# First lists' products deferred, later lists a step later, residual loads on the stores' queue, the last block in pieces, more strip buffers: a graph layer on one Trainium2 core

## The chip, the cores and the metric

One core of a Trainium2 chip. The metric is device time of one execution in microseconds (us). The four executions of a kernel mostly lie within 1% of each other. Every experiment was checked against the reference (all correct) and timed in turn with the kernel before on the same chip. The experiments ran in five batches on five chips (median of before 1692.8 to 1701.8), so a difference of a few us across batches means little.

## The reference

```python
def reference(x, adj, W):                  # x (8, 4096, 256), adj (4096, 4096), W (256, 256), all f32
    A = relu((adj + adj.T) * 0.5)
    D = A.sum(axis=1)
    r = where(D > 0, D, 1) ** -0.5          # 0 where D is 0
    L = eye(4096) - r[:, None] * A * r[None, :]
    y = relu(einsum('nm,bmo->bno', L, einsum('bnf,fo->bno', x, W)))
    z = x + y
    return (z - mean(z)) / sqrt(var(z) + 1e-5)   # over the last axis
```

`adj` is sparse, so the kernel gathers only the rows it needs.

## The kernel before

Phase one goes over blocks of A (8 x 8 of 512 x 512): transpose, add, store to `a_dram`; between them `form(m)` makes G = r·xW for 128 rows. It also makes the first lists of gather indices. Phase two has 15 full units and a half one; a unit computes two blocks of 128 output rows, b0 and b1, with four PSUM banks each. Its products use gathered tiles of A (`ga`) and G (`g`). Each list is ready two units ahead.

```python
    # phase one, at the end of a row i of blocks (cut)
    for u in ([0], [1, 2], [3])[i]:
        patterns(u)                          # VectorE: kinds
        tot = psum.tile(..., tag="b0"); low = psum.tile(..., tag="b0")
        count(u, tot, low)                   # TensorE: products over kinds
        place(u, tot, low)                   # VectorE

    # form(m) (cut): all transposes and copies of a block first, then all its products
    for b in range(0, B, 2):
        ...transpose x[b], x[b + 1]; nc.scalar.copy(xt[:, b : b + 2], pt)
    for b in range(0, B, 2):
        ...products of xt with W

    # phase two (cut)
    def residual(i, ypool):
        xr = ypool.tile([P, B, F], F32, tag="xr", name=f"xr_{i}", bufs=4)
        nc.scalar.dma_start(xr, x[...block i...])
        return xr

    def finish(i):
        y = evict(i, py.pop(i), ypool)       # ScalarE: relu(-r * PSUM), four banks
        def rest():
            mv, rstd = moments(i, y, xr.pop(i), stat)     # VectorE: z = xr + y, statistics
            def end():
                normalise(i, z, mv, rstd)    # VectorE; then the store on SyncE's queue
                if i + 3 < NB:
                    xr[i + 3] = residual(i + 3, ypool)
            after(6, end)
        after(1, rest)

    def lists(u):
        one = psum.tile([P, S], F32, tag="b0"); two = psum.tile([P, S], F32, tag="b0")
        count(u + 4, ...); count_rest(u + 3, ...)
        collect(u + 2, pl); index(u + 2, pl)              # 32 small products; VectorE reads them
        place_rest(u + 3, ...); place(u + 4, ...)         # VectorE reads the rest of both banks

    for q, (u, step) in enumerate(steps):    # a step: the products of one or two gathered pairs
        ...
        finish(2 * u + 1 + b)                # when block b has had its last product
        if b == 0:
            after(2, lists, u)               # two steps later
```

The lists of a unit take two of the four `b0` banks, and the first products of the next unit need all four. A load of `xr` goes into the buffer of four blocks earlier and so waits for that block's store to land. VectorE does its work in program order, so an add that waits for a residual holds up the reads of the lists behind it.

## Time and profile before

| | before |
|---|---|
| median of 4 runs, us | 1696.8 (1692.9 to 1702.0) |
| first product of phase two | 630.8 |
| first list's products to the sixth's ("five units") | 740 to 1091: 351 us |
| first to last product of phase two | 1031 us |
| last product to the end | 29.5 us |

The times inside are from the timeline of the profiled run. "Five units" runs from the lists' products of unit 0 to those of unit 5.

### The profile page before, as it was taken

To read this page: it belongs to the slowest core of one execution; us is meant where nothing else is said; L and a number is where in the kernel's file an instruction comes from. 1 tells how busy PE (TensorE), PEld (TensorE's weight loads), DVE (VectorE), ACT (ScalarE), POOL (GpSimd) and SP (SyncE) were. 2 spreads that over 40 slices of the span, in tenths; PEclk is the share of its full clock that TensorE was granted. 3 is DMA by queue.
4 is the path that set the end of the run, shared out by engine and by line. 5 is a ranking of instruction groups with operands and counts; after the bars stand their busy time and mean duration, and the time that the engine had idled before them with its cause. 6 is when DMAs were issued, how large, how long until landed. Compare 5 with 4: busy or idle time off the path is not lost.

```text
span 1691.1 us, 18475 instructions
## 1 busy us (share of the span) xinstructions
PE 1517.8 (90%) x6544; PEld 802.7 (47%) x6544; DVE 802.6 (47%) x1831; ACT 360.7 (21%) x453; POOL 818.9 (48%) x1113
## 2 busy tenths in 40 slices
PE   6999779598898979999999999999997999988693
PEld 5887657486776723434343333333332333333231
DVE  4776676758455320051507154446436336415325
ACT  3655435354443510010100001001101101100110
POOL 3010010101011146667677777777777778768550
PEclk8999979799998989999999999999998999989897
DMA  9999979898997679989898999999998999999984
GB/s 334 375 383 388 387 279 393 305 396 323 335 323 257 235 283 401 353 300 359 334 358 316 380 354 366 389 359 352 372 359 296 383 348 350 353 369 339 332 334 152
DMA packets 229156, 575.13 MB, mean 340 GB/s; under 512 B 19913, under 2 KB 118521, under 8 KB 191385
## 3 DMA queue, kind: packets, MB, share of 16 engines
q0 software_dynamic: 56672, 305.12, 47.1%
q1 hardware_dynamic: 100352, 134.23, 23.0%
q10 hardware_dynamic: 72032, 134.51, 21.2%
q8 instruction: 55, 0.90, 0.2%
q14 instruction: 45, 0.37, 0.1%
HBM read 479.07 MB, written 136.34 MB: 364 GB/s over the span
## 4 chain that ended last, share of the span: by engine, by line
PE 38%; DMA 23%; issue 22%; DVE 11%; POOL 4%; ACT 1%; ACTq 0%; POOLq 0%; SPq 0%; DVEq 0%
PE py L693 15%; DMA out_dram<-xr 13%; PE pg L425 10%; DMA xr<-in_x_dram 9%; PE lead L396 6%; PE tr L341 4%; PE xtr L415 3%; DVE xr L536 2%; DVE xr L522 2%; DVE stats L527 2%; POOL ga L588 1%; DVE hot L263 1%; DMA g<-g_dram,gi 1%; POOL g L598 1%; DVE part L346 1%
## 5 line engine op out<-in xcount | busy, mean ns | idle before, releaser
L693 PE MATMUL py<-g,ga 128*64 128x512 f32 (+1 forms) x3152 | 959.2, 606 | 34.4 <-issue 15.6
L693 PEld LDWEIGHTS py<-g,ga 128*64 128x64 f32 (+1 forms) x3152 | 359.5, 155 | 622.2 <-issue 593.5
L598 POOL DMA_INDIRECT g<-g_dram,gi x302 | 358.8, 1188 | 188.0 <-PE py L693 76.3
L588 POOL DMA_INDIRECT ga<-a_dram,ai x302 | 333.1, 1103 | 100.0 <-issue 81.9
L522 DVE TENSOR_TENSOR xr<-xr,y 128x2048 f32<-128x2048 f32 x32 | 73.3, 2289 | 521.6 <-ACT y L512 300.3
L512 ACT ACTIVATE y<-py,minus_r 128x512 f32<-128x512 f32 x124 | 78.0, 687 | 964.7 <-PE py L693 428.4
L344 DVE TENSOR_TENSOR sym<-tr,adj 128x512 f32<-128x512 f32 x256 | 158.6, 681 | 209.0 <-PE tr L341 142.3
L425 PE MATMUL pg<-w_sb,xt 128*128 128x256 f32 x1024 | 232.1, 383 | 1.4 <-ACT xt L416 1.2
L425 PEld LDWEIGHTS pg<-w_sb,xt 128*128 128x128 f32 x1024 | 194.0, 193 | 32.1 <-ACT xt L416 4.2
L391 POOL DMA_DIRECT2D strip<-a_dram x32 | 18.7, 587 | 321.5 <-PE lead L396 302.5
L341 PE MATMUL tr<-ident,adj 128*128 128x128 f32 x1024 | 135.3, 288 | 30.0 <-DMA adj<-in_adj_dram 12.8
L346 DVE TENSOR_REDUCE part<-sym 128x32 f32<-128x2048 f32 x64 | 144.1, 2275 | 7.9 <-ACT sym L345 7.8
L345 ACT ACTIVATE sym<-sym 128x2048 f32<-128x2048 f32 x64 | 122.5, 1913 | 113.9 <-DVE sym L344 113.8
L341 PEld LDWEIGHTS tr<-ident,adj 128*128 128x128 f32 x1024 | 120.7, 148 | 44.3 <-issue 19.0
L536 DVE TENSOR_SCALAR xr<-xr,mv,rstd 128x256 f32<-128x256 f32 x256 | 86.7, 410 | 85.7 <-POOL rstd L534 85.7
L434 ACT ACTIVATE gt<-pg,r 128x512 f32<-128x512 f32 x96 | 66.0, 687 | 100.4 <-PE pg L425 100.3
L527 DVE BATCH_NORM_STATS2 stats<-xr 128x6 f32<-128x256 f32 x256 | 86.8, 410 | 0.7
L396 PE MATMUL lead<-gt,strip 128*128 128x512 f32 x192 | 86.5, 592 | 0.0
L366 POOL TENSOR_TENSOR r<-e,neg_half 128x4 f32<-128x4 f32 x8 | 8.3, 1043 | 154.9 <-DVE e L365 154.9
L416 ACT COPY xt<-xtr 128x512 f32<-128x512 f32 x128 | 67.8, 591 | 71.2 <-PE xtr L415 71.0
L415 PE MATMUL xtr<-ident,xin 128*128 128x128 f32 x512 | 73.7, 297 | 9.1 <-DVE sym L344 8.0
L534 POOL TENSOR_TENSOR rstd<-rstd,neg_half 128x8 f32<-128x8 f32 x32 | 59.0, 1843 | 33.9 <-DVE rstd L530 33.3
(100 smaller groups left out, 587.0 us busy)
## 6 DMA issues: line engine op xcount, KB each, us to landing
adj<-in_adj_dram SPq DMA_DIRECT2D x64, 1024.0 KB
a_dram<-sym ACTq DMA_DIRECT2D x64, 1024.0 KB
xin<-in_x_dram SPq DMA_DIRECT2D x32, 1024.0 KB
xr<-in_x_dram ACTq DMA_DIRECT2D x32, 1024.0 KB
out_dram<-xr SPq DMA_DIRECT2D x32, 1024.0 KB
g_dram<-gt ACTq DMA_DIRECT2D x24, 1024.0 KB
g_dram<-held ACTq DMA_DIRECT2D x8, 1024.0 KB
ga<-a_dram,ai POOLq DMA_INDIRECT x302
```

Of the source, the lines that this page charges most:

```text
L341: nc.tensor.transpose(pt[:, c * P : (c + 1) * P], tji[:, c, a * P : (a + 1) * P], ident)
L344: nc.vector.tensor_add(sym[:, a, :], pt, tij[:, a, :])
L345: nc.scalar.activation(sym, sym, AF.Relu, scale=0.5)
L346: nc.vector.tensor_reduce(part[:, i * A : (i + 1) * A, j * S // Q : (j + 1) * S // Q], sym.rearrange("p a (c q) -> p a c q", q=Q), AX.X, A ...
L396: nc.tensor.matmul(lead[c], lhsT=strip, rhs=g[:, c * S : (c + 1) * S], start=not done, stop=len(done) == NB - 1, skip_group_check=True,)
L415: nc.tensor.transpose(pt[:, k, c, :], xin[:, b + k, c * P : (c + 1) * P], ident)
L425: nc.tensor.matmul(pg[:, k * FO : (k + 1) * FO], lhsT=xt[:, b + k, c, :], rhs=w_sb[:, c, :], start=(c == 0), stop=(c == FC - 1),)
L527: nc.vector.bn_stats(stats[:, b, :], z[:, b, :])
L536: nc.vector.tensor_scalar(z[:, b, :], z[:, b, :], mv[:, b, 0:1], rstd[:, b : b + 1], ALU.subtract, ALU.mult,)
L588: nc.gpsimd.indirect_dma_start(out=at if both else at[:, :P], out_offset=None, in_=a_pairs if both else a_rows, in_offset=bass.IndirectOff ...
L598: nc.gpsimd.indirect_dma_start(out=gt, out_offset=None, in_=g_dram, in_offset=bass.IndirectOffsetOnAxis(ap=gi[:, t : t + 1], axis=0), boun ...
L693: nc.tensor.matmul(py[2 * u + 1 + b][c][rows, :], lhsT=at[:, off + rows.start : off + rows.stop], rhs=gt[:, c * S : (c + 1) * S], start=ne ...
```

## The change

Intent: TensorE shall not wait for the first lists' kinds at row ends (the products are put some blocks behind); ScalarE's evictions shall not stand behind residual loads that wait for stores (these loads go to SyncE, which issues the stores, and the lists come a step later); the tail shall overlap (four pieces); GpSimd shall fetch strips earlier (eight buffers). The diff, cut to its core:

```diff
-            t = xpool.tile([P, P], F32, tag="strip", name=f"strip_{m}", bufs=4)
+            t = xpool.tile([P, P], F32, tag="strip", name=f"strip_{m}", bufs=8)
...                                            # form(): transposes of b beside products of b - 2
-            for b in range(0, B, 2):
-                ...transposes, copy into xt[:, b : b + 2]
-            for b in range(0, B, 2):
+            xts = {}
+            for b in range(0, B + 2, 2):
+                if b < B:
+                    ...transposes
+                    xts[b] = xpool.tile([P, 2, FC, P], F32, tag="xt", name=f"xt_{m}_{b}", bufs=3)
+                    nc.scalar.copy(xts[b], pt)
+                b -= 2
+                if b < 0:
+                    continue
+                xt = xts.pop(b)
...                                            # after every block of A: run_due()
+                    due.append([2 + n, count_place, (u,)])
+                    due.append([1 + u, count_place_rest, (u,)])
+                due.append([2, collect_index, (i - 4,)])
...
-        nc.scalar.dma_start(xr, x[:, i * P : (i + 1) * P, :].rearrange("b p f -> p b f"))
+        nc.sync.dma_start(xr, x[:, i * P : (i + 1) * P, :].rearrange("b p f -> p b f"))
...
+            if i == NB - 1:
+                finish_last(i)                 # per PSUM bank: evict, add, statistics, normalise, store
+                return
...
-                        after(2, lists, u)
+                        after(3, lists, u)
```

## The prediction

> **What bounds the kernel now.** I read the page first, then the windows table in stretches of 100 and of 20 us, then the waits, and last the timeline around each gap. The kernel has two phases. Until about 620 us it symmetrises A, stores it, forms G = r·xW and makes the first index lists; after that it gathers rows of A and G with 302 pairs of indirect transfers and multiplies them. The windows (columns: TensorE, weight loads, VectorE, ScalarE, GpSimd busy; granted clock; DMA share; GB/s):
>
> ```profile
> 100.00:200.00 100.00, 96.20 (x546) 79.17 (x546) 64.66 (x88) 52.58 (x64) 8.77 (x17) 0.98 1.04 386
> 200.00:300.00 100.00, 78.75 (x436) 62.26 (x436) 68.92 (x99) 43.67 (x45) 6.48 (x13) 0.88 0.92 343
> 500.00:600.00 100.00, 93.22 (x464) 70.57 (x463) 41.75 (x63) 41.84 (x52) 13.71 (x26) 0.95 0.72 262
> 1000.00:1200.00 200.00, 197.89 (x810) 75.48 (x809) 89.79 (x267) 15.39 (x24) 154.30 (x130) 1.00 0.97 370
> 1400.00:1600.00 200.00, 167.53 (x596) 65.27 (x594) 88.36 (x266) 17.07 (x28) 145.34 (x121) 0.91 0.94 349
> ```
>
> TensorE and DMA are near their limits together. From 100 to 200 us TensorE is 96% busy and the DMA moves 386 GB/s; the best 20 us windows of the whole run show 400 to 409, and I use 392 as a sustained ceiling. From 380 to 620 us TensorE alone binds (262 GB/s). The middle of phase two has both full; its end (1400 to 1600) has 32 us without a matmul, at 349 GB/s. So the reader should see that a removed wait pays only where the other limit has room.
>
> The gaps of phase one are the ends of rows of blocks. There TensorE stands in program order before the count of a list:
>
> ```profile
> 209.54 2.48 DVE L344 TENSOR_TENSOR sym<-tr,adj 128x512 f32<-128x512 f32 x4 [3.17 <-DMA a_dram<-sym]
> 221.30 0.47 PE L206 MATMUL tot<-kind,ones 128*128 128x352 bf16 x1 [16.41 <-DVE kind L196]
> PE tot L206 <- DVE kind L196: 36.7, 4, 18.7
> ```
>
> VectorE itself was held by a full set of sym buffers whose stores had not landed, so the count's input came late. In phase two ScalarE's queue issues the residual loads, and each waits there until an output store has landed; the evictions behind it wait too:
>
> ```profile
> 1499.93 15.29 ACTq L506 DMA_DIRECT2D xr<-in_x_dram  x2
> 1515.33 2.42 ACT L512 ACTIVATE y<-py,minus_r 128x512 f32<-128x512 f32 x4 [54.19 <-DMA xr<-in_x_dram]
> 1516.06 0.18 PE L234 MATMUL lists<-rest,ones 128*128 128x32 bf16 x1 [7.42 <-ACT y L512]
> 1524.14 2.29 DVE L522 TENSOR_TENSOR xr<-xr,y 128x2048 f32<-128x2048 f32 x1 [36.43 <-DMA xr<-in_x_dram]
> 1530.54 44.64 PE L693 MATMUL py<-g,ga 128*64 128x512 f32 x128 [5.06 <-DVE pos_r L171]
> ```
>
> Two stalls in one unit: 7.4 us because the eviction stood behind the second load, and 5.1 us because VectorE, waiting for the first load to land, read the lists' PSUM late. The tail:
>
> ```profile
> 1661.88 0.37 ACTq L506 DMA_DIRECT2D xr<-in_x_dram  x1
> 1662.36 2.42 ACT L512 ACTIVATE y<-py,minus_r 128x512 f32<-128x512 f32 x4 [18.55 <-PEq L725]
> 1673.62 2.29 DVE L522 TENSOR_TENSOR xr<-xr,y 128x2048 f32<-128x2048 f32 x1 [9.70 <-DMA xr<-in_x_dram]
> 1681.22 2.67 DVE L536 TENSOR_SCALAR xr<-xr,mv,rstd 128x256 f32<-128x256 f32 x8 [1.82 <-POOL rstd L534]
> ```
>
> The last matmul ends near 1662.3 and the span 28.8 us later, of which 9.7 are the wait for the last residual.
>
> **What the Trainium skill says.** "DMA: Bandwidth & Descriptors", section "Queues, rings and completion order": SP and ACT own one row of rings each on the same 16 engines, and each engine takes turns between rows, packet by packet. The trace agrees in kind: a 1 MB output store alone on its row took 17.8 us (1482.1 to 1499.9) beside the gathers, far below an equal share of bytes. Section "Anatomy of one DMA — SWDGE (gpsimd) path": the wait for a semaphore happens on the issuing sequencer. The trace shows it, 15.3 us on ScalarE's queue. "TensorE: Matmul & The Clock Gate", section "What's actually happening": half clock after an idle window. After the stall ending at 1530.5 weight loads come every 0.86 us, and from 1536.4 every 0.43, so a stall costs about 3 us more than its length. "SBUF — State Buffer", section "SBUF: two separate sides": VectorE can lock GpSimd out of its port while descriptors are written. One gather issue took 4.47 us beside the 4.42 us hot comparison, 0.94 otherwise. The change leaves that as it is.
>
> **Part one: lists' products later.** Idle TensorE time at row ends, from the 20 us windows: row one (180 to 240 us) 20.9, row two (280 to 320) 18.7, rows three to five 5.3, 7.8 and 6.8. After rows one and two the DMA has to have room: 220 to 260 us ran at 197 and 345 GB/s, which against 392 is 9.9 + 2.4 = 12.3 us; 300 to 340 at 317 and 269, 3.8 + 6.3 = 10.1 us. In rows three to five TensorE binds and all 19.9 us could go. Cap: 42 us. I take 60%, 25 us: VectorE still waits for the sym stores, the four PSUM banks stay full until it has added, and a deferred count now takes two of these banks in the middle of a row. Against it stands the new order in form(): the first product follows two transposes, not four. The transpose began at 185.44 and ScalarE's first copy ended at 186.65, so the product can start at about 186.75, where the two transposes are through at 186.3: 0.44 us of idle per form. For some 18 forms after 380 us, where TensorE binds, that is 8 us. Net 17.
>
> **Part two: residual loads on SP; lists a step later.** In favour: the ScalarE stall goes. TensorE waited for evictions before lists 12.6 + 10.0 + 7.4 + 1.1 = 31.1 us, and each stall costs a ramp. But at the cited unit the second limit ends at the same 1530: VectorE has to have the residual first. It lands 24.2 us after issue, issue follows the store of four blocks earlier, and that follows a normalisation which stands behind the previous residual add in VectorE's order. This loop took 66 us from add to add (1476.6 to 1542.6); a unit has 57 us of DMA work (16 tiles of 1.13 MB and 4.2 MB at 392 GB/s). The change lengthens it: the instruction order of SP now reads store, load (waits for that store), store, load. A second store, formerly issued 5.6 us after the first, waits until the first has landed, about 12 us, and its load follows it on a row that moves about 60 GB/s under gathers. The loop becomes about 75 us where gathers keep running; when TensorE stalls they stop, and the row speeds up. I expect the first stall to go, the second to stay, and a few late units to gain or lose 3 us: 6 us won in the whole phase.
>
> **Part three: last block in pieces.** After the last matmul, for each of four pieces: eviction 0.69, add 0.57, two statistics 0.82, aggregate and epsilon 0.33, GpSimd power about 1.6 with its waits, two normalisations 0.67. VectorE's share of the four is about 10 us, and the order shows five of block 29's eight normalisations and all of block 30's behind it, 13 × 0.33 = 4.3 us, which formerly came ahead. Their stores, 2 MB, end the program: about 6 us. So 0.7 + 10 + 4.3 + 6 = 21, plus up to 4 us for a residual that still arrives late: 23 against 28.8. Gain 6.
>
> **Part four: eight strips.** GpSimd waited 302.5 us for a strip's slot, but it had nothing else to do; only at 602 us did the power of r stand behind strips, and TensorE lost 0.6 us. Worth 0 to 1.
>
> Sum: 1694.6 − 17 − 6 − 6 − 0.5 = **1665 us**, 1.7% less.
>
> **Rivals.** (a) Evictions were the real brake. ScalarE's waits on stores and residuals (235 and 203 us) speak for it, and the 54 us of idle TensorE in phase two with their ramps. Then phase two gains up to 35 us, limited by DMA, and the time is about 1636. Against: units late in the run already take 58 to 62 us by their evictions, near the 57 of DMA. (b) SP becomes the bound: stores and loads share one row and one waiting sequencer. Then the late units take 5 to 8 us more each, seven of them give back 40 us, and the time is about 1700. Against: the rows get faster whenever gathers pause. (c) DMA hides part one: the saved stalls of rows one and two return as waits for blocks of A. Then part one is worth 8 us and the time 1674.
>
> **Range and chances.** The parts' spreads are about 10, 18 and 5 us, together about 22 us; 80% is 1632 to 1692. The 2% line lies at 1660.7, a little under my middle: faster 0.45, same 0.50, slower 0.05.
>
> **What would show it.** Right: no TensorE wait of 16 us for a kind; phase two starting 12 to 22 us earlier; small TensorE waits for the xt copy at each form; evictions directly after their matmuls, with TensorE waits before products still on VectorE reads of lists, and SP issues held 10 us or more by stores; about 23 us after the last matmul. Wrong: late units under 56 us or over 66, a tail over 28, or a wait for blocks of A as long as the old one for kinds.

## More of the kernel before

Most of the reading is in the prediction; only the hardware queues are added here (packets, MB, share of the 16 engines' time; q10 holds ScalarE's transfers and q1 SyncE's):

```profile
q1 hardware_dynamic: 100352, 134.23, 23.0%
q10 hardware_dynamic: 72032, 134.51, 21.2%
```

## The result

After: 1761.97 us, median of 4 runs (1754.2 to 1765.0), against 1696.76 of the kernel before: ratio 1.0383 (1.0339 to 1.0428). It is 3.8% **slower**, and outside the range.

| | before | after |
|---|---|---|
| first product of phase two | 630.8 | 627.7 |
| five units | 351 | 369 |
| first to last product of phase two | 1031 | 1095 |
| last product to the end | 29.5 | 29.3 |

Phase one is 3 us shorter, the tail the same, and all the loss is in phase two. The page's queues show the loads moved over:

```profile
q1 hardware_dynamic: 133680, 167.78, 28.4%
q10 hardware_dynamic: 38752, 100.96, 14.7%
```

The waits of the kernel after (what waited, for what: us in all, times, longest), TensorE in phase two and then SyncE's queue over the run:

```profile
PE py L738 <- DVE pos_k L170: 35.2, 5, 13.7
PE py L738 <- DVE low L299: 17.9, 1, 17.9
PE py L738 <- DVE pos_r L245: 17.4, 1, 17.4
```

```profile
SPq L531 <- DMA out_dram<-xr: 409.8, 23, 41.1
```

The waits for evictions ahead of lists (31 us before) are gone, as intended, and so is the 36.7 us wait for kinds. In their place TensorE waits 76.1 us for VectorE's reads of the lists (70.5 in the rows shown, 5.6 in two smaller ones), against 15.1 before (8.3 for `pos_k`, 5.1 for `pos_r`, 1.7 for `low`). SyncE stands 410 us in front of residual loads, waiting for stores. One stall of after, in the timeline (start, duration, engine, what, and in brackets the idle time before it and what ended it):

```profile
1563.97 0.19 PE L234 MATMUL lists<-rest,ones 128*128 128x32 bf16 x1
1564.92 1.94 PE L738 MATMUL py<-g,ga 128*64 128x512 f32 x8
1569.89 3.61 PE L738 MATMUL py<-g,ga 128*64 128x512 f32 x6 [3.03 <-DVE pos_r L171]
1587.84 2.29 DVE L548 TENSOR_TENSOR xr<-xr,y 128x2048 f32<-128x2048 f32 x1 [18.00 <-DMA xr<-in_x_dram]
1590.05 0.17 DVE L298 COPY low<-lists 128x16 f32<-128x16 f32 x1
1590.87 4.67 PE L738 MATMUL py<-g,ga 128*64 128x512 f32 x14 [17.37 <-DVE pos_r L245]
```

Read it from below: TensorE's products waited 17.4 us for VectorE to read the lists, which stood behind an add, which waited 18 us for its residual. Four of TensorE's waits are of this kind, 52 us in all. Four others (1194 to 1388 us, 24 us in all) follow no late residual: there VectorE copies the list 8 to 10 us late, of which more below. The same list in the kernel before:

```profile
1517.59 7.89 PE L693 MATMUL py<-g,ga 128*64 128x512 f32 x24
```

Before, 24 products as the profile counts them (7.9 us) lay between the lists' products and the first product that needs their banks. After, 8 (1.9 us) do: "a step later" spends that slack. SyncE's order, in the same kernel:

```profile
1527.31 0.38 SPq L571 DMA_DIRECT2D out_dram<-xr  x1
1539.60 0.37 SPq L531 DMA_DIRECT2D xr<-in_x_dram  x1
1540.02 0.58 SPq L571 DMA_DIRECT2D out_dram<-xr  x1
```

The load of 1539.60 waited for a store to land, and the store of 1540.02 stood behind it, though its normalisation ended at 1534.9: the serialisation that the prediction had read from the instruction order.

### The profile page after: what moved, and what is told of

Read it like the earlier page. It is cut to its first block, busy times and chain, and to the rows that moved or that the text cites. A ratio compares the mean times of both kernels' runs of the same rounds, so it can differ in the third digit from the quotient of the medians.

```text
span 1752.4 us, 18499 instructions
## 1 busy us (share of the span) xinstructions
PE 1546.2 (88%) x6544; PEld 808.5 (46%) x6544; DVE 800.6 (46%) x1837; ACT 363.0 (21%) x453; POOL 812.9 (46%) x1116
## 4 chain that ended last, share of the span: by engine, by line
PE 60%; DMA 13%; issue 11%; DVE 10%; POOL 2%; ACT 2%; another core or an unknown queue 2%; SPq 0%; ACTq 0%; DVEq 0%; POOLq 0%
PE py L738 43%; PE pg L430 10%; DMA out_dram<-xr 7%; PE lead L396 4%; DVE sym L344 3%; DMA xr<-in_x_dram 2%; PE xtr L420 2%; ACT sym L345 1%; DVE part L346 1%; PE tr L341 1%; DVE xr L563 1%; DVE xr L548 1%; DVE stats L553 1%; DMA a_dram<-sym 1%
## 5 line engine op out<-in xcount | busy, mean ns | idle before, releaser
L738 PE MATMUL py<-g,ga 128*64 128x512 f32 (+1 forms) x3152 | 980.4, 608 | 104.4 <-DVE pos_k L170 35.2
L738 PEld LDWEIGHTS py<-g,ga 128*64 128x64 f32 (+1 forms) x3152 | 367.5, 155 | 708.9 <-issue 644.7
L625 POOL DMA_INDIRECT g<-g_dram,gi x302 | 374.2, 1239 | 257.2 <-PE py L738 167.8
L615 POOL DMA_INDIRECT ga<-a_dram,ai x302 | 316.8, 1049 | 101.5 <-issue 83.4
L548 DVE TENSOR_TENSOR xr<-xr,y 128x2048 f32<-128x2048 f32 (+1 forms) x35 | 73.7, 2105 | 490.4 <-ACT y L537 298.8
L430 PE MATMUL pg<-w_sb,xt 128*128 128x256 f32 x1024 | 253.0, 397 | 26.2 <-ACT xt L422 18.7
L344 DVE TENSOR_TENSOR sym<-tr,adj 128x512 f32<-128x512 f32 x256 | 162.4, 683 | 124.3 <-PE tr L341 108.5
L391 POOL DMA_DIRECT2D strip<-a_dram x32 | 17.4, 545 | 336.0 <-PE lead L396 328.4
L396 PE MATMUL lead<-gt,strip 128*128 128x512 f32 x192 | 92.2, 594 | 1.6 <-DMA strip<-a_dram 1.6
L422 ACT COPY xt<-xtr 128x512 f32<-128x512 f32 x128 | 73.3, 580 | 16.6 <-PE xtr L420 16.1
L420 PEld LDWEIGHTS xtr<-ident,xin 128*128 128x128 f32 x512 | 62.9, 145 | 29.9 <-DVE sym L344 17.3
```

What stands on the lines that cost most here:

```text
L344: nc.vector.tensor_add(sym[:, a, :], pt, tij[:, a, :])
L396: nc.tensor.matmul(lead[c], lhsT=strip, rhs=g[:, c * S : (c + 1) * S], start=not done, stop=len(done) == NB - 1, skip_group_check=True,)
L420: nc.tensor.transpose(pt[:, k, c, :], xin[:, b + k, c * P : (c + 1) * P], ident)
L430: nc.tensor.matmul(pg[:, k * FO : (k + 1) * FO], lhsT=xt[:, k, c, :], rhs=w_sb[:, c, :], start=(c == 0), stop=(c == FC - 1),)
L615: nc.gpsimd.indirect_dma_start(out=at if both else at[:, :P], out_offset=None, in_=a_pairs if both else a_rows, in_offset=bass.IndirectOff ...
L625: nc.gpsimd.indirect_dma_start(out=gt, out_offset=None, in_=g_dram, in_offset=bass.IndirectOffsetOnAxis(ap=gi[:, t : t + 1], axis=0), boun ...
```

## The experiments

Theory at the start: lists a step later and loads on SyncE, because of late residuals. Rivals: lists a step later by itself; SyncE's queue by itself; a slower TensorE. Labels with `a_` undo parts of after, with `b_` add parts to before; `d_only` is the kernel before with the deferral alone. All outputs are right.

### Undoing part two, half by half

```diff
 # a_act: after, loads back on ScalarE      # a_two: after, lists back at two steps
-        nc.sync.dma_start(xr, ...)          -                        after(3, lists, u)
+        nc.scalar.dma_start(xr, ...)        +                        after(2, lists, u)
 # a_act_two: both.   b_sp: before, with nc.sync.dma_start(xr, ...) alone
```

> The changed kernel with its residual loads back on ScalarE's queue, all else kept. Theory Q (the shared SP queue is the loss: a store waits in the queue until the load ahead of it may be issued, and its own load then comes later): about 1700 us, near the kernel before. Theory L (the lists a step later are the loss: their PSUM is read by VectorE behind the second residual add, and the next block's products wait for that): still about 1745 us. If the two feed one another, between the two.

> The changed kernel with the lists back at two steps after the block, residual loads still on SP. Theory Q: still about 1745 us, with second stores of a unit held behind loads. Theory L: about 1700 us, and no TensorE wait of 10 us or more for VectorE's reads of the lists. If they feed one another, both this and the ScalarE variant get back most of the 65 us.

> Both undone: the changed kernel keeps only the deferred first products, the reordered form, the strips and the last block in pieces. If the loss is all of phase two's, 1680 to 1700 us; with what I predicted of the first phase and the tail, about 1672 us. If it stays over 1730 us, neither Q nor L is the cause.

> The kernel before with the residual loads on SP alone. Theory Q: 1730 us or more. Theory L: 1690 to 1705 us. If the queue matters only together with the later lists, 1695 to 1715 us.

Measured (before 1701.75): a_act 1753.55 (1.0297), a_two 1709.31 (1.0009; median of its three fast runs), a_act_two 1703.26 (1.0003), b_sp 1720.3 (1.0085). So lists a step later cost 53 us (a_two to after) and 50 us (a_act_two to a_act); the loads on SyncE cost 8 (a_act to after), 6 (a_act_two to a_two) and 19 us (before to b_sp), by the ratios 15, 1 and 14, which is near the scatter. Neither half brings a gain.

The waits do not divide like the times. The largest of a_two, TensorE in phase two:

```profile
PE py L738 <- DVE pos_k L170: 40.3, 3, 20.7
PE py L738 <- DVE low L299: 25.8, 1, 25.8
```

In all TensorE waits for reads of the lists 5.8 us in a_act_two, but 70.6 in a_two, 66.3 in a_act and 89.1 in b_sp. Either half alone brings these waits, while only the step later costs some 50 us. So their sum is not the loss.

### The same halves from the other side, and the deferral alone

```diff
 # b_three: before, with
-                        after(2, lists, u)
+                        after(3, lists, u)
 # b_three_s6: b_three, and the even blocks' add put off so that VectorE reads the lists first
-            after(1, rest)
+            after(1 if i % 2 else 6, rest)
-                after(6, end)
+                after(6 if i % 2 else 1, end)
 # a_five: after, and
-  xr bufs=4;  ga in a pool of RING + 2
+  xr bufs=5;  ga bufs=RING
 # d_only: after with old form(), 4 strips, old tail, loads on ScalarE, lists at two
```

> The kernel before with the lists one step later, alone. From the first batch (the changed kernel lost about 50 us with the lists at three steps whichever queue the loads used) this should be 1745 us or so, with TensorE waits of 10 us and more for VectorE's reads of the lists in the late units. If it stays under 1710 us, the step costs only together with the rest of the change.

> As the run before, but the residual add of each unit's second block is put off (its normalisation stays where it was), so that VectorE's order reads the lists ahead of it, as in the kernel before; the lists are still a step later on TensorE. If the order on VectorE is what costs (reads of the lists behind a second wait for a residual), about 1700 us. If the later place on TensorE is what costs (no products between the lists and the next block), still about 1745 us.

> The changed kernel with five residual buffers in place of four (the small gathered tiles have 13 buffers in place of 15 to make room). A load then needs the store of five blocks earlier, which has long landed. If late residuals are the root of both losses, about 1700 us or less, with hardly any wait for residuals on VectorE. If the shared queue's bandwidth is the root, still about 1750 us.

> The kernel before with the deferred first products alone (old form, four strips, old tail, loads on ScalarE, lists at two). My first part said 25 us of the first phase for this alone: 1675 us, and first products of phase two at about 606 us against 630.8. If the blocks of A limit the rows' ends, or the reordered waits come back elsewhere, 1695 to 1700 us.

Measured (before 1698.24): b_three 1708.31 (1.0040), b_three_s6 1705.18 (1.0038), a_five 1701.28 (0.9994), d_only 1681.33 (0.9892). Lists a step later cost only 10 us on top of before, against some 50 in after, though TensorE waits 70.6 us for reads of the lists in b_three too. Putting the adds off changes nothing, but it is no test of VectorE's order, since the edit did not do what it was meant to: in the trace of b_three_s6 the copy of a late list still stands behind an add that waits for its residual, and TensorE's waits for the lists stay at 63.6 us:

```profile
1548.60 2.29 DVE L522 TENSOR_TENSOR xr<-xr,y 128x2048 f32<-128x2048 f32 x1 [13.12 <-DMA xr<-in_x_dram]
1550.81 0.17 DVE L298 COPY low<-lists 128x16 f32<-128x16 f32 x1
```

A fifth residual buffer takes back all 60 us, but not by making the residuals early: with the loads on SyncE, VectorE's adds still wait 130 us for them (after 128) and TensorE 70.8 us for the lists. What changed with it is the slow stretch that is described below: a_five does not have it (five units 338 us against 369). The deferral alone is a gain of 1.1%: phase two starts at 613.8 instead of 630.8.

### What makes the same step cost 10 us in one kernel and 50 in another

```diff
 # a_form: after with the old order in form() and 4 strips
 # a_tail: after without "if i == NB - 1: finish_last(i); return"
 # d_three: d_only with after(3, lists, u)
 # d_five: d_only with xr bufs=5, ga bufs=RING
```

> After, with the old order inside form() and four strips; deferral, loads on SyncE, lists at three and the tail pieces stay. Phase two has the same instructions as after. Theory one (late residuals cost the 60 us): phase one gets some 15 us shorter as in d_only, phase two stays, 1740 to 1750. Rival (the loss of the first five units is TensorE's slow stretch after the lists' products, 0.7 us for a pair of products and then the half clock, which comes or stays away with the timing of the build: there in before and after, away in d_only, b_three and a_five): 1740 or more if the stretch stays, 1700 to 1720 if it goes, and the wait of the copy of low for TensorE in units one to five tells which.

> After, with the last block finished whole again. Nothing ahead of the last unit changes, so both theories expect the first five units as in after (84, 78, 73, 67, 67 us). The tail in pieces was predicted to be worth 6 us; it ends 29 us after the last product in before and after alike, so I expect 1760 to 1768.

> The deferral alone (d_only) with lists at three. Theory one (a later list collides with late residuals whatever stands ahead): as in b_three, 5 to 10 us more than d_only, 1685 to 1692. Rival (the slow stretch after lists decides): 1685 to 1692 if no unit among the first five shows the copy of low waiting 7 us for TensorE, 1710 to 1730 if they do.

> The deferral alone with five residual buffers, paid for by a smaller ring of gathered blocks of A (13). Theory one: late residuals make VectorE and TensorE wait in units six to thirteen of d_only too, so 1655 to 1675, better than any so far. Rival (five buffers only moved the slow stretch away in a_five, which d_only does not have): 1678 to 1690.

Measured (before 1695.35): a_form 1748.07 (1.0295), a_tail 1761.28 (1.0390), d_three 1730.02 (1.0195), d_five 1670.14 (0.9844).

The tail in pieces is worth nothing (1761.3 against 1762.0). The new form() costs 14 us, and they lie in phase one: its first product of phase two comes at 627.7, in a_form at 612.7. (The two profiled executions, a_form's slowest and after's fastest, span the same 1752 to 1753 us, because phase two took 1110 us in a_form's.) TensorE, weight loads, VectorE, ScalarE, GpSimd busy, clock, DMA share and GB/s in the first 180 us, of a_form and of after:

```profile
0.00:180.00 180.00, 161.37 (x911) 134.40 (x912) 111.60 (x144) 92.06 (x111) 22.60 (x393) 0.96 1.01 371
```

```profile
0.00:180.00 180.00, 152.99 (x872) 126.98 (x873) 110.99 (x144) 88.31 (x105) 24.79 (x397) 0.97 1.00 358
```

TensorE loses 8 us where I had taken the DMA to be the limit. A typical wait for the `xt` copy is 0.56 us (I had worked out 0.44), but there are 20 of them, 18.7 us in all against 1.2 us before. (One of 7.3 us, at 27 us, is no loss: a_form's first product comes as late.)

d_three is the surprise: the same step costs 49 us on top of d_only. Yet d_three and b_three (and a_act up to its tail) have **the same instructions in phase two**: I compared the compiled programs, and order, waits and semaphores agree on all five engines. Only the PSUM banks differ, and before and b_three, with the same banks, differ in what follows too. They differ in what TensorE does after the lists' 32 small products, in each of the first five units. Here 4 us windows of b_three and of d_three, beginning 2 to 3 us after the products of the second list (columns as above):

```profile
828.00:832.00 4.00, 4.00 (x22) 1.43 (x20) 4.00 (x19) 0.00 (x0) 3.09 (x4) 1.00 1.02 416
832.00:836.00 4.00, 4.00 (x22) 1.30 (x19) 4.00 (x4) 0.00 (x0) 3.69 (x2) 1.00 1.02 420
```

```profile
812.00:816.00 4.00, 2.68 (x7) 0.74 (x7) 0.15 (x1) 0.00 (x0) 3.02 (x4) 1.00 1.02 422
816.00:820.00 4.00, 2.20 (x7) 0.41 (x5) 0.00 (x0) 0.00 (x0) 1.97 (x2) 1.00 1.01 416
```

22 products in 4 us become 7 (some records may be missing), with no semaphore wait shown, at the full granted clock and the same DMA traffic. I call this the slow stretch. VectorE sees it too, since its copy of the list comes late (b_three, then d_three):

```profile
827.76 0.15 DVE L298 COPY low<-lists 128x21 f32<-128x21 f32 x1
```

```profile
820.81 0.18 DVE L298 COPY low<-lists 128x21 f32<-128x21 f32 x1 [8.67 <-remote]
```

The copy stays late beyond the first five units: in nine lists of d_three (6.7 to 9.5 us) and ten of after (5.9 to 10.0), even where the products run at their usual rate (after at 1246 us: 24 in 7.3 us, the copy 10.0 us late). In a_act the stretch of one unit is long enough for the granted clock to fall to 0.50 behind it (908 to 910 us), so it is paid twice. Before, after, a_act, a_two, a_act_two, b_sp, a_form, a_tail, d_three and d_five have the stretch in most of the first five units; d_only, b_three, b_three_s6 and a_five do not.

### Buffers, the burst of small products, and the place in TensorE's stream

```diff
 # d_three_p64, d_only_p64: at the start of the program
+    idle = psum.tile([P, P], F32, tag="b1", name="idle")
+    for _ in range(64):
+        nc.tensor.transpose(idle, ident, ident)
 # d_five_split: d_five, in lists()
-                collect(u + 2, pl)                    # 32 small products
-                index(u + 2, pl)
+                collect(u + 2, pl, range(NB // 2))    # 16; the other 16 and index() one step later
+                after(1, second)
 # d_five_three: d_five with after(3, lists, u)
```

> d_three (1730, slow stretch in five units) with 64 idle transposes at the start of TensorE's stream; the order of everything else in phase two is the same. Theory stream (the slow stretch is TensorE's instruction supply, and depends on where the lists' burst falls in the stream): the set of units with the stretch changes, and if it goes, 1690 to 1700. Theory chance of timing: the same as d_three plus at most 10 us from the transposes, 1728 to 1742, with the stretch in the same units.

> d_only (1681, no slow stretch) with the same 64 idle transposes. Theory stream: the stretch may appear in the first five units, 690 to 1700 in that case meaning 1690 to 1700. Theory chance of timing: no stretch, 1680 to 1692.

> d_five (1670, slow stretch in four units, lists at two) with the 32 small products of a list issued in two halves of 16, one step apart. Theory burst (64 TensorE instructions within 1 us outrun their supply): the stretch goes or halves, 1655 to 1665. Theory lists as such (something else in the lists' step): the stretch stays, 1668 to 1678.

> d_five with lists at three. Late residuals as the cause of the 50 us: 1668 to 1680, since five buffers take them away. The slow stretch as the cause: 1690 to 1705 if the stretch is there in the first five units (they then take about 369 us), and 1665 to 1675 if it is not (about 339 us).

Measured (before 1692.75): d_three_p64 1721.07 (1.0137), d_only_p64 1676.87 (0.9896), d_five_split 1699.52 (1.0032), d_five_three 1669.53 (0.9833).

The idle transposes brought the stretch into d_only: its copies of `low` now wait 4.2 to 7.9 us, and its five units go from 340 to 352 us. They did not take it out of d_three. So it depends on something as small as TensorE's stream ahead of it, or on the 2.6 us by which phase two moved; what it waits for stays open. Lists at two do not lose by it: d_only_p64 ends no later than d_only. Lists at three do: d_only_p64 to d_three_p64, one batch with the stretch in both, is 44 us. The split was a failure as a test: in the unit that I looked at TensorE still slowed down, and the second half came so late that TensorE waited 4.7 us for its reading (eleven such waits, 63 us in all).

d_five_three is decisive on one point: the stretch alone does not make the step dear. It has the stretch (five units 366 us), and still lists at three cost nothing on top of d_five, against 49 us with four buffers. TensorE's and VectorE's waits in phase two, d_three:

```profile
PE py L730 <- DVE pos_k L170: 39.7, 5, 22.6
PE py L730 <- DVE low L299: 13.8, 1, 13.8
PE py L730 <- DVE pos_r L245: 12.3, 1, 12.3
```

```profile
DVE xr L543 <- DMA xr<-in_x_dram: 94.7, 4, 36.3
```

and d_five_three, where no add of VectorE waits for a residual at all:

```profile
PE py L730 <- DVE pos_k L170: 14.4, 5, 9.5
PE py L730 <- DVE low L299: 3.7, 1, 3.7
PE py L730 <- DVE pos_r L171: 2.8, 1, 2.8
```

### The queue with five buffers, and a sixth

```diff
 # a_five_act: a_five with nc.scalar.dma_start(xr, ...)
 # d_six: d_five with xr bufs=6, RING = 12 and ga bufs=RING
```

> After with five residual buffers and the loads back on ScalarE's queue; lists at three, the new form(), eight strips and the tail in pieces stay. It differs from d_five_three (1669.5) by the new form(), which cost 15 us of phase one, and from a_five (1701) by the queue. Loads on SyncE cost 9 to 19 us also here: 1682 to 1692. Loads on SyncE cost nothing once five buffers are there: 1697 to 1705.

> d_five (1670) with six residual buffers and a ring of 12 instead of 13 gathered rows of G. Late residuals still bind: 1655 to 1665. They do not any more (VectorE's adds waited for no residual load in the windows of d_five): 1668 to 1680, the shorter ring costing a few us.

Measured (before 1697.76): a_five_act 1674.80 (0.9883), d_six 1644.25 (0.9696). Neither has the stretch. The loads on SyncE cost 26 us also where five buffers are there (1701.3 against 1674.8, two batches; 19 us by the ratios); 1674.8 is outside what I expected. **d_six is the best version, 3.0% faster than before** (interval 0.9650 to 0.9743). I had expected no gain from the sixth buffer, since VectorE's adds waited for no load in d_five. That was the wrong row: ScalarE's evictions stood behind loads whose buffer waited for a store. d_five and then d_six, phase two:

```profile
ACT y L532 <- DMA out_dram<-xr: 249.0, 5, 56.8
```

```profile
ACT y L532 <- DMA out_dram<-xr: 123.8, 3, 56.9
```

How much of the 26 us between the two is the buffer and how much the absent stretch, these runs do not separate.

### Phase two at a glance

First to last product, us, from the profiled runs (single executions, before's being one of its fastest, so a difference of 10 us means little); loads on ScalarE:

| | four buffers | five | six |
|---|---|---|---|
| lists at two, stretch | before 1031, a_act_two 1037, d_only_p64 1043 | d_five 1039 | |
| lists at two, none | d_only 1041 | | d_six 1012 |
| lists at three, stretch | d_three 1097, d_three_p64 1094, a_act 1095 | d_five_three 1039 | |
| lists at three, none | b_three 1053, b_three_s6 1047 | a_five_act 1020 | |

And with the loads on SyncE: a_two 1060 and b_sp 1072 (lists at two), after 1095, a_tail 1105 and a_form 1110 (three), a_five 1047 (three, five buffers, no stretch).

Where the time went, in the same runs: the five units, the rest of phase two from the sixth list's products on, and TensorE's waits for VectorE's reads of the lists.

| | five units | the rest | waits for the lists |
|---|---|---|---|
| before (two, ScalarE) | 351 | 571 | 15 |
| d_only (two, ScalarE, no stretch) | 340 | 592 | 15 |
| b_sp (two, SyncE) | 349 | 614 | 89 |
| b_three (three, ScalarE, no stretch) | 338 | 602 | 71 |
| d_three (three, ScalarE) | 371 | 613 | 71 |
| after (three, SyncE) | 369 | 614 | 76 |
| a_five (three, SyncE, five buffers, no stretch) | 338 | 597 | 71 |
| d_five (two, ScalarE, five buffers) | 350 | 580 | 2 |
| d_five_three (three, ScalarE, five buffers) | 366 | 560 | 21 |

Lists at three lengthen the five units by some 15 to 18 us where the stretch is there, and in after TensorE waits for no list in them; without the stretch they lengthen nothing. In the rest, with four buffers, either half costs some 20 to 45 us and both together hardly more (after 43, a_form 55); with five buffers and the loads on ScalarE the step costs nothing. Waits of some 70 us stand in kernels from 1701 to 1762 us: they show where TensorE stood, not what the change cost.

## Why the prediction was wrong

The terms, measured by runs that differ in that alone:

| term | predicted | measured |
|---|---|---|
| deferral of the first products | −25 | −17 (before to d_only) |
| new form() | +8 | +14 (a_form to after; with the strips) |
| lists a step later | part two, −6 in all | +44 to +53 (a_two to after, a_act_two to a_act, d_only to d_three, d_only_p64 to d_three_p64); +10 on before alone; 0 with five buffers (d_five to d_five_three) |
| loads on SyncE | in the same −6 | +6 to +26 (by the ratios +1 to +19) |
| tail in pieces | −6 | about 0 (a_tail to after) |
| strips | −0.5 | not measured by themselves |

A chain of four kernels adds up to the result: before 1.000, deferral 0.989 (d_only), lists at three 1.020 (d_three), loads on SyncE and tail pieces 1.030 (a_form), new form() and strips 1.038 (after).

**The step that failed is part two:** "I expect the first stall to go, the second to stay, and a few late units to gain or lose 3 us: 6 us won in the whole phase." Its mechanism was seen rightly: the first stall went, SyncE does serialise stores and loads, and the second stall is VectorE behind a late residual. But the second stall did not stay, it grew: from 15.1 us of TensorE's waits for the lists to 76.1. Either half of part two brings it there by itself (a_two 70.6, a_act 66.3, against 5.8 with both undone); the prediction counted the 31 us that go and held constant what comes. In time it is the step later that costs, 44 to 53 us with four buffers where the stretch is there.

What I left out is the price of "a step later": it spends the slack between the lists' products and the reuse of their banks (7.9 us to 1.9 in the list shown). With that gone, whatever is late there stops TensorE. Two things are: residual adds, since a buffer comes back only after four blocks (52 of the 76 us), and VectorE's late copy of the list (24). That the first is needed for the loss is shown: without late adds the step costs nothing (d_five_three). With late adds and no stretch it costs 10 us (b_three), so the loss of some 50 was seen only where both are there. How they act together is argued: at three, the stretch goes with some 45 us more of phase two with four buffers and some 19 with five (10, if both runs are brought to their medians); at two, with nothing that shows. These are single executions of kernels that differ in more than the stretch.

**Rival (b)**, SyncE as the bound at about 1700, was the right direction and too small; I set its chance low. It is shown apart from lists at three: b_sp is 0.85% slower, a_five 26 us (by the ratios 19) slower than a_five_act. Rival (a), evictions as the real brake, is refuted for this change: they now follow their products at once, and phase two got longer. Rival (c), DMA hides part one, falls too: d_only keeps its 17 us.

**Part one** erred in two terms that both went the wrong way. The deferral gave 17 instead of 25. For form() I counted "some 18 forms after 380 us" and nothing ahead, because the DMA was near its limit there; TensorE lost 8 us in the first 180 us nevertheless. (The reading that TensorE alone binds from 380 us on was too wide as well: 262 GB/s is the rate from 500 us; from 380 to 500 it was 323, with TensorE 89% busy.) So phase two started 3 us earlier, not 12 to 22. **Part three** gave nothing: 29.3 us after the last product against 29.5, where I predicted 23. The block's first add came 5.6 us after the end of the last product, since it waited for the last residual; from that add to the last normalisation took 15.2 us and the stores 7.9, where I had 0.7 and up to 4, 14.3 and 6. In a_tail, where the block is finished whole, add to normalisation took 10.7 us and the tail 24.0: the pieces lengthened what they were to shorten, while 9.7 us of before's tail were a wait for the residual.

Of the marks that the prediction set, the missing wait for kinds, small waits for the `xt` copy, evictions right after their products and SyncE held for 10 us or more (409.8 us in 23 waits) came true; 23 us after the last product and a phase two 12 to 22 us earlier did not. Two of its signs of being wrong came: late units over 66 us (68 to 70 in three of the later ones of after) and a tail over 28.

**What stays open:** what TensorE waits for in the slow stretch. 64 idle transposes at the start brought it, and two kernels with the same instructions in phase two differ in it; its being TensorE's instruction supply is a guess that no run shows. The packets of the instruction queue q8 in the kept traces do not settle it: one block of 16 KiB comes 1.2 us after the list's first product both in d_three (810.4 us, stretch) and in b_three (827.0, none). Open too are why VectorE's copy of the list comes late, and why some 70 us of waits for the lists cost 10 us in b_three.

## What to carry to other kernels

Before moving work later in order to dodge one wait, count the slack up to the next user of its buffers: here 6 us of slack were spent to save waits of 31 us, and the kernel lost some 50. A load that has to wait for its buffer holds up whatever stands behind it in its queue, on either engine; another buffer took the wait away with the loads on ScalarE (d_five_three) but not on the stores' queue (a_five), and another queue only moved it. The sixth residual buffer, paid for with a slot of the gather ring, is in the fastest version. A sum of waits is not a cost: kernels with the same 70 us of waits differ by 60 us in time. An edit has to be checked in the trace for what it was meant to do (b_three_s6 did not do it). And a change in parts has to be measured in parts: the deferral alone, 1.1% faster, was buried under the rest.

## What the Trainium skill lacked or had wrong

- "DMA: Bandwidth & Descriptors", section "Issuing engines are not separate DMA queues", says that issuing from several engines only saves the sequencer's time to initiate. It leaves out that the queue in which a load *waits* matters more here: the same 32 loads on the stores' engine cost 0.85% on the kernel before (b_sp) and 19 to 26 us in after with five buffers, with SyncE's queue standing 409.8 us at loads that wait for stores in after. (That the wait stands on the issuing sequencer is in another section of the page, which the prediction cites.)
- "Runtime: NRT & Kernel Launch", section "Instruction fetch mechanics", has instructions fetched in blocks of 16 KiB by the engine's own queue, mostly hidden. The block size agrees (the instruction queue q8 of d_five: 55 packets, 0.90 MB). No page has the slow stretch after 64 TensorE instructions within 1 us: products at about a third of their rate for 6 to 8 us without a semaphore wait, present or absent with the same instructions, and going with 28 to 33 us of five units when lists stand at three (338 us without it, 366 to 371 with it).
